# Reordering router, gather and scatter steps around TensorE's work in an attention and mixture-of-experts kernel

## The chip, the cores and the metric

The kernel runs on one core of one Trainium2 chip. The metric is the device time of one execution in microseconds (us). Five engines matter: TensorE (PE, its weight loads shown apart as PEld), VectorE (DVE), ScalarE (ACT), GpSimd (POOL) and SyncE (SP, which here only issues DMAs).

## What is computed

The input is `x` with 8 batches of 1024 tokens of 512 features, in fp32. Two residual steps follow each other:

```
x = x + attention(layernorm(x))      # 16 heads of 32 features; q, k, v are cos/sin of scaled inputs
x = x + moe(layernorm(x))            # 8 experts, 2 per token, at most 160 slots per expert and batch
```

In the attention, q and k are `[cos, sin]` of `x / (1+|w|) + b + t*phi`, v is `cos + sin` of `x / (1+|w|) + b`; the scores are causal and go through a softmax, and the output passes through another `cos + sin`. In the mixture of experts a router (`x @ Wr`, softmax, top 2) gives each token two experts and two gates. Each choice gets a slot, in token order, of its expert and batch; choices past slot 160 are dropped. An expert computes `relu(x @ W1 + b1) @ W2 + b2` (512 to 2048 to 512) on its 8 * 160 = 1280 slots, and each token adds up its two results times their gates.

## The kernel before: how the work is tiled and in which order it runs

**Attention.** The main loop (L1274) runs over n = 0 to 31: batch b = n // 4, and c = n % 4, a chunk of 128 features, which is four heads in two pairs. An iteration prepares q and k for a later chunk, makes the scores of the pairs (`scores`, L658; matmul at L667, exp on ACT at L687), multiplies by v (`attend`, L693; matmul at L701, eviction by DVE at L709) and turns the result back to tokens (`turn`, L725). The order of the instructions on PE, ACT, DVE and SP is written by hand (`manual_schedule`): Python generators are advanced a step at a time, and what is emitted first stands first in the engine's queue. POOL's order is chosen by the framework's own scheduler.

The steps that the change moves:

- `qk_pre(n)` (L492): 16 transposes on PE into a PSUM tile of two banks, and four DVE operations (L508) that scale and add into `qk_f`. The pool of such tiles, `ps_sc`, has three buffers, which scores, router and turns share.
- `v_post(n)` (L622): one DVE product (L436) that writes the v tile; `v_pre` prepares the next one.
- `router(b-1)` (L754) is advanced through batch b's iterations by `route_on`. It makes mean and scale of each token (L765, `inverse_root`), then works on groups g = 0 to 3 of two token tiles: `rows(t)` (L773) normalizes a tile of 128 tokens on DVE (L775) and has SP store it to DRAM (`xn2_d`, L781; its pool `row2` has two buffers); `features(g)` (L786) transposes two rows on PE and copies them out to `xT` (L802 on DVE, L794 on ACT for the last batch) and then calls `rows` for the next group; `sums(g)` multiplies by the router weights (L838), and adds up the parts of the group before (L821). Then come the choice of experts, the counting of places (`mask`, `prior` L903 to L906, matmuls through L821) and `slot` and `token` tiles (L926, L931).
- In the iteration after c == 0, `begin` is true: the router of the batch before starts at the end of iteration c == 0, and `qk_pre` for the next chunk is emitted in the first half of iteration c == 1.

**From router to experts.** `scatter` (L746) writes 16 lists of 128 (token, gate) pairs to `slot_d[b]`, each by an indirect DMA from POOL (L749). `fetch_slots(b)` (L948) reads the slot table back into `slots` (L954). `find_rows(i)` (L1022) turns it into row numbers (`source`), for the first 768 slots of each expert (i = 0, batches 0 to 4) or the other 512 (i = 1). `gather(i)` (L1031) fetches 128 rows at a time by an indirect DMA from POOL (L1037, pool `gp` of two buffers), has PE transpose them (L200 for the first chunk, L1054 later), and forms sums and differences of quarters for Strassen's scheme on DVE.

**Experts.** There are 16 chunks, two per expert (768 and 512 rows). A chunk runs eight `layer1(i, q)` (L1088; seven products each, matmul at L1098) and then two or three `layer2` blocks (L1134; seven products each, matmul at L1143). `mix_w1` (L1074) forms the differences of W1's quarters, on POOL for the first chunk and on DVE later; `mix_w2` (L1001) those of W2 on DVE (L1007 to L1010). `layer2` sends each finished tile of 128 rows to the output by an accumulating indirect DMA from POOL (`send`, L1165). SP loads W1 two steps ahead (`load_ahead`, three buffers) and W2 once per expert.

**The passage between the two.** In the last iteration (n = 31) `experts_begin` (L1199) calls `find_rows(0)`, loads W1 and runs `gather(0)` beside the attention. The last batch's output stage and router (`ending`, L1419) are advanced one step after each layer 1 product of the first chunk, by `next(ending)`. After `layer1(0, 4)` what is left of `ending` is emitted at once, and W2's loads follow on SP. The next chunk's gather is advanced one step after each layer 2 product (`aside`).

Of the kernel before, what the change touches and what calls it, by code (L numbers as in the profile page):

```python
# [21 lines left out]
P = 128  # L22
# [51 lines left out]
def preln_attn_moe_kernel(  # L74
# [667 lines left out]


    scatters = []

    def scatter():  # L746
        while scatters:
            b, idx, src = scatters.pop(0)
            nc.gpsimd.indirect_dma_start(  # L749
                out=slot_d[b], out_offset=bass.IndirectOffsetOnAxis(ap=idx, axis=0),  # L750
                in_=src, in_offset=None,
            )

    def router(b):  # L754

# [7 lines left out]
        mv = small.tile([P, NTT, nc.vector.BN_AGGR_DIM], F32, name="mv")  # L763
        for t in range(NTT):
            nc.vector.bn_aggr(mv[:, t, :], stats[:, t, :, :].rearrange("p c s -> p (c s)"))  # L765
        rstd = inverse_root(mv[:, :, 1], "rstd")

        copy = nc.scalar.copy if b == B - 1 else nc.vector.tensor_copy
        prob = once.tile([P, NTT, E], F32, name="prob")
# [3 lines left out]
        def rows(t):  # L773
# [10 lines left out]
        last = b == B - 1  # L784

        def features(g):  # L786

            xT = row2.tile([P, NCH, 2 * P], F32, name="xT", bufs=1)
            if last:
                for i, xn in enumerate(ahead):  # L790
                    ps = pools["ps_tr"].tile([P, NCH, P], F32, name="ps_t")
                    for c in range(NCH):
                        nc.tensor.transpose(ps[:, c, :], xn[:, c * P : (c + 1) * P], ident)
                    copy(xT[:, :, i * P : (i + 1) * P], ps)  # L794
            else:
                ps = two_banks()
                for i, xn in enumerate(ahead):
                    for c in range(NCH):
                        at = (NCH * i + c) * 64
                        by_halves(ps[:, :, at : at + 64], xn[:, c * P : (c + 1) * P])  # L800
                for a in range(2):
                    copy(  # L802
                        xT.rearrange("p c (i a q) -> p i c a q", a=2, q=64)[:, :, :, a, :],
                        ps[:, a, :].rearrange("p (i c q) -> p i c q", i=2, q=64),
                    )
            if g + 1 < NTT // 2:
                ahead[:] = [rows(2 * g + 2), rows(2 * g + 3)]
                if not last and 2 * g + 4 == NTT:
                    store()
            return xT  # L810

        def one_bank():
            if last:
# [134 lines left out]
    def fetch_slots(b):  # L948

        rows = slot_d[b][: E * CAP, :].rearrange("(e c) k -> c e k", e=E)  # L950
        s0 = b * CAP
        while s0 < (b + 1) * CAP:
            s1 = min((s0 // P + 1) * P, (b + 1) * CAP)
            nc.gpsimd.dma_start(  # L954
                meta[s0 % P : s0 % P + s1 - s0, :, s0 // P, :],
                rows[s0 - b * CAP : s1 - b * CAP],
            )
            s0 = s1


# [70 lines left out]
    def gather(i):  # L1031

        e, j0, nh = chunks[i]
        xe = pools["xep"].tile([P, NCH, 2, HALF], F32, name="xe")
        for j in range(2 * nh):
            xg = pools["gp"].tile([P, D], F32, name="xg")
            nc.gpsimd.indirect_dma_start(  # L1037
                out=xg, out_offset=None, in_=xn2_d[i % 2],
                in_offset=bass.IndirectOffsetOnAxis(ap=source[:, e, j0 + j, None], axis=0),
            )  # L1040
            yield None
            dst = xe[:, :, j // nh, j % nh * P : (j % nh + 1) * P]
            if i == 0:
                ps = two_banks()[:, :, : NCH * 64]
                for c in range(NCH):
                    by_halves(ps[:, :, c * 64 : (c + 1) * 64], xg[:, c * P : (c + 1) * P])
                nc.vector.tensor_copy(
                    dst.rearrange("p c (a q) -> p c a q", a=2),
                    ps.rearrange("p a (c q) -> p c a q", q=64),
                )  # L1050
            else:
                ps = pools["ps_tr"].tile([P, NCH, P], F32, name="ps_t")
                for c in range(NCH):
                    nc.tensor.transpose(ps[:, c, :], xg[:, c * P : (c + 1) * P], ident)  # L1054
# [10 lines left out]
        yield a11, a12, s4, a22, a21, s2, s3  # L1065

    def start(gen, box):
        for box[0] in gen:
            yield
# [4 lines left out]
    def mix_w1(i, q):  # L1074
# [59 lines left out]
    def layer2(i, block, hs, aside):  # L1134
# [27 lines left out]
            )  # L1162

        def send(r):
            nc.gpsimd.indirect_dma_start(  # L1165
                out=out,
                out_offset=bass.IndirectOffsetOnAxis(ap=meta[:, e, jj[r], 0:1], axis=0),
                in_=ys[r], in_offset=None, compute_op=ALU.add,
            )

        p1, u2, u3 = temp("p1"), temp("u2"), temp("u3")
        nc.scalar.copy(p1, product(0, 0))  # L1172
# [26 lines left out]
    def experts_begin():  # L1199

        for name, bufs in (("w1p", 3), ("t1p", 2), ("xep", 1), ("tmp_p", 2), ("gp", 2)):
            pools[name] = to_end.pool(name, bufs, **right)
        find_rows(0)
        for k in range(AHEAD):
            load_ahead(k)
        yield from start(gather(0), first_parts)
        mix_w1(0, 0)

    def experts(ending):
        pools["hp"] = to_end.pool("hp", NHQ, **right)  # L1210
        pools["ps_tr"] = to_end.pool("ps_tr", 2, space=PSUM)
        pools["ps_p"] = to_end.pool("ps_p", 6, space=PSUM)
        box = first_parts
        mixes = loads = iter(())
        for i, (e, j0, nh) in enumerate(chunks):
            parts, box = box[0], [None]
            hs = []
            for q in range(NHQ):
                load_ahead(i * NHQ + q + AHEAD)
                some(3, loads)  # L1220
                if q + 1 < NHQ:
                    mix_w1(i, q + 1)
# [14 lines left out]
            aside = start(gather(i + 1), box) if i + 1 < len(chunks) else iter(())  # L1237
            for block in range(nh):
# [32 lines left out]
    o_st = route = first_rows = None  # L1271
    begin = False
    place, angles, residual = [None], iter(()), iter(())
    for n in range(NCK):  # L1274
# [52 lines left out]
        route_on(1)  # L1327
        route_on(1)
        rest(angles)
        if more:  # L1330
            v_st = v_box[0]
# [9 lines left out]
        if late:  # L1341
            turn(1, halves1, pos)
            o_st = o_pre(n - 1, pos)
        route_on(1)
        if n == 2:
            load_b1()
# [35 lines left out]
        if begin:  # L1382
            rest(residual)
            route = router(b - 1)
            next(route)
        elif n + 2 < NCK:
            qk_st = rest(qk_pre(n + 2))

        if c != 1:
            next(residual, None)  # L1390
        route_on(1)
        if n + 2 < NCK and not begin and c != 1:
            angle(*qk_st)
        if c != 1:
# [24 lines left out]
    def ending():  # L1419
# [4 lines left out]
        square(o_st[0])  # L1424
        for _ in range(3):
            yield
        rest(o_post(NCK - 1, o_st))
        for _ in range(3):
            yield
        for name in router(B - 1):  # L1430
# [39 lines left out]
```

## Time and profile before

| | |
|---|---|
| median of 3 runs | 3331.85 us (3321.11 to 3336.68) |
| the profiled execution: time | 3330.72 us |
| the profiled execution: span | 3329.0 us |
| TensorE busy, share of the span | 3203.4 us, 96% |
| VectorE busy | 2272.0 us, 68% |
| mean granted TensorE clock | 0.990 |
| 0 to 1311 us | attention |
| 1311 to 1412 us | layer 1 of the first chunk, with the last batch's router |
| from 1412 us | layer 2 of the first chunk, then the other 15 chunks |

A line of the timeline gives start, duration, engine, source line, operation, what it writes and reads, its shape and the count of merged instructions; in brackets stands how long the engine was idle before it and what ended that. A line of the waits gives the waiting instruction, what it waited for, the total in us, how often, and the longest. A busy PE may still be slow: its clock can be granted at less than full speed.

### The profile page before, as it was taken

To read this page: it belongs to the slowest core of one execution; us is meant where nothing else is said; L and a number is where in the kernel's file an instruction comes from. 1 tells how busy PE (TensorE), PEld (TensorE's weight loads), DVE (VectorE), ACT (ScalarE), POOL (GpSimd) and SP (SyncE) were. 2 spreads that over 40 slices of the span, in tenths; PEclk is the share of its full clock that TensorE was granted. 3 is DMA by queue.
4 is the path that set the end of the run, shared out by engine and by line. 5 is a ranking of instruction groups with operands and counts; after the bars stand their busy time and mean duration, and the time that the engine had idled before them with its cause. 6 is when DMAs were issued, how large, how long until landed. Compare 5 with 4: busy or idle time off the path is not lost.

```text
span 3329.0 us, 48774 instructions
## 1 busy us (share of the span) xinstructions
PE 3203.4 (96%) x18942; PEld 2172.0 (65%) x18942; DVE 2272.0 (68%) x4975; ACT 1320.9 (40%) x1617; POOL 429.5 (13%) x397
## 2 busy tenths in 40 slices
PE   3999999999999998899999999999999999999998
PEld 1444444444444444588688688688688688688687
DVE  7887878788787675746746846845845845845854
ACT  5788888878787874201101201201201201201201
POOL 2000202020111103321011011011011011011010
PEclk8999999999999999999999999999999999999999
DMA  4445353545535342422322322322322422322321
GB/s 133 117 121 168 106 165 101 167 134 147 174 106 153 87 143 78 126 39 73 111 38 71 114 42 64 117 39 64 117 45 58 121 42 61 119 46 61 114 39 26
DMA packets 234462, 319.74 MB, mean 96 GB/s; under 512 B 21640, under 2 KB 154488, under 8 KB 222200
## 3 DMA queue, kind: packets, MB, share of 16 engines
q1 hardware_dynamic: 211232, 273.37, 27.8%
q0 software_dynamic: 22912, 43.22, 7.4%
q8 instruction: 150, 2.46, 0.3%
q14 instruction: 80, 0.66, 0.1%
q10 hardware_dynamic: 88, 0.02, 0.0%
HBM read 187.62 MB, written 61.82 MB: 75 GB/s over the span
## 4 chain that ended last, share of the span: by engine, by line
PE 59%; DVE 2%; DMA 1%; issue 0%; ACT 0%; POOL 0%; SPq 0%; POOLq 0%; DVEq 0%; ACTq 0%
PE ps_p L1143 28%; PE ps_p L1098 28%; PE av L701 1%; PE ps_t L1054 1%; PE ps_s L667 1%; DMA out_dram<-y,slots 0%; DMA xg<-xn_d,source 0%; DMA xn_d<-xn 0%; DMA w<-in_L_ffn_W_dram 0%; DVE y L1159 0%; PE ps_s L200 0%; DVE w_t L1009 0%; DVE w L1008 0%; DVE t L1083 0%; DVE u L1185 0%
## 5 line engine op out<-in xcount | busy, mean ns | idle before, releaser
L687 ACT ACTIVATE e<-ps_s 128x1024 f32<-128x1024 f32 (+1 forms) x640 | 567.8, 938 | 212.0 <-PE ps_s L667 130.8
L667 PE MATMUL ps_s<-qk 64*128 64x512 f32 (+3 forms) x3072 | 599.4, 508 | 48.5 <-DVE qk_f L508 20.2
L1143 PE MATMUL ps_p<-w,hid 128*128 128x256 f32 x2560 | 569.6, 380 | 0.0
L1143 PEld LDWEIGHTS ps_p<-w,hid 128*128 128x128 f32 x2560 | 484.6, 190 | 66.3
L701 PE MATMUL av<-e,v 128*64 128x512 f32 (+3 forms) x3072 | 526.6, 492 | 0.0
L1143 PE MATMUL ps_p<-w_t,hid 128*128 128x256 f32 x1920 | 430.3, 379 | 0.6 <-DVE w_t L1009 0.6
L667 PEld LDWEIGHTS ps_s<-qk 64*128 64x128 f32 x3072 | 263.3, 189 | 233.3 <-issue 109.4
L1143 PEld LDWEIGHTS ps_p<-w_t,hid 128*128 128x128 f32 x1920 | 361.8, 190 | 48.7 <-DVE w_t L1009 1.0
L701 PEld LDWEIGHTS av<-e,v 128*64 128x64 f32 x3072 | 201.4, 137 | 285.1 <-issue 269.5
L1098 PE MATMUL ps_p<-xe_s,t 128*128 128x256 f32 (+1 forms) x1024 | 299.3, 435 | 4.3 <-DVE t L1083 3.4
L1098 PE MATMUL ps_p<-xe,w 128*128 128x256 f32 (+1 forms) x1024 | 301.8, 438 | 1.1 <-issue 1.1
L1098 PE MATMUL ps_p<-xe,t 128*128 128x256 f32 (+1 forms) x1024 | 296.8, 433 | 0.0
L749 POOL DMA_INDIRECT slot_d<-token,slot x128 | 161.1, 1259 | 1014.1 <-issue 697.3
L1172 ACT COPY p<-ps_p 128x256 f32<-128x256 f32 x40 | 14.8, 369 | 612.9 <-PE ps_p L1143 612.9
L1098 PEld LDWEIGHTS ps_p<-xe_s,t 128*128 128x128 f32 x1024 | 194.4, 191 | 89.4 <-DVE t L1083 7.9
L1098 PEld LDWEIGHTS ps_p<-xe,w 128*128 128x128 f32 x1024 | 194.8, 192 | 83.9 <-issue 4.9
L1098 PEld LDWEIGHTS ps_p<-xe,t 128*128 128x128 f32 x1024 | 194.4, 190 | 80.9 <-issue 0.4
L1037 POOL DMA_INDIRECT xg<-xn_d,source x80 | 78.1, 976 | 1102.8 <-PE ps_t L1054 1020.9
L1165 POOL DMA_INDIRECT out_dram<-y,slots x80 | 126.3, 1579 | 661.8 <-DVE y L1160 522.4
L1113 ACT ACTIVATE p<-ps_p,b_t 128x256 f32<-128x256 f32 (+1 forms) x128 | 65.4, 511 | 330.7 <-DVE y L1159 169.7
L1117 ACT ACTIVATE hid<-hid 128x256 f32<-128x256 f32 (+1 forms) x128 | 60.1, 470 | 321.7 <-DVE hid L1116 321.7
L1130 ACT ACTIVATE hid<-hid,b_more 128x256 f32<-128x256 f32 (+1 forms) x128 | 71.8, 561 | 271.5 <-DVE hid L1129 271.5
(217 smaller groups left out, 3844.8 us busy)
## 6 DMA issues: line engine op xcount, KB each, us to landing
w<-in_L_ffn_W_dram SPq DMA_DIRECT2D x256, 256.0 KB
w<-in_L_ffn_W_dram SPq DMA_DIRECT2D x64, 512.0 KB
qk<-qk_c SPq DMA_DIRECT2D x124, 256.0 KB
qk<-qk_r SPq DMA_DIRECT2D x124, 256.0 KB
qk_base<-base_d SPq DMA_DIRECT2D x28, 1024.0 KB
xn_d<-xn SPq DMA_DIRECT2D x72, 256.0 KB
x_mid<-in_L_attn_x_dram SPq DMA_DIRECT2D x16, 1024.0 KB
out_dram<-x_mid SPq DMA_DIRECT2D x8, 2048.0 KB
```

The lines of the kernel that those rows point to most:

```text
L667: nc.tensor.matmul(ps[:, a, at : at + w], lhsT=pair[r, 1, kb * P : (kb + 1) * P], rhs=pair[r, 0, q0 : q0 + w], start=at == 0, stop=not own ...
L687: nc.scalar.activation(e, ps[:, :, :n], AF.Exp, scale=UNIT * UNIT / math.sqrt(2 * DH))
L701: nc.tensor.matmul(av[a * 64 : (a + 1) * 64, q0 - 512 * h :], lhsT=vt[:, kb, 2 * pr + a, :], rhs=es[i][:, a, at : at + w], start=kb == 0, ...
L749: nc.gpsimd.indirect_dma_start(out=slot_d[b], out_offset=bass.IndirectOffsetOnAxis(ap=idx, axis=0), in_=src, in_offset=None,)
L1037: nc.gpsimd.indirect_dma_start(out=xg, out_offset=None, in_=xn2_d[i % 2], in_offset=bass.IndirectOffsetOnAxis(ap=source[:, e, j0 + j, None ...
L1054: nc.tensor.transpose(ps[:, c, :], xg[:, c * P : (c + 1) * P], ident)
L1098: nc.tensor.matmul(ps, lhsT=weights[:, k, :], rhs=rows[:, k, :], start=k == 0, stop=k == 1)
L1113: nc.scalar.activation(p1, product(b11, a11), AF.Identity, bias=b1_t[:, e * NHC + q : e * NHC + q + 1])
L1117: nc.scalar.activation(h11, h11, AF.Relu)
L1130: nc.scalar.activation(h12, h12, AF.Relu, bias=more)
L1143: nc.tensor.matmul(ps, lhsT=hs[k][:, part, cols], rhs=ws[k][weight], start=k == 0, stop=k == NHQ - 1,)
L1165: nc.gpsimd.indirect_dma_start(out=out, out_offset=bass.IndirectOffsetOnAxis(ap=meta[:, e, jj[r], 0:1], axis=0), in_=ys[r], in_offset=None ...
```

## The change

Seven edits are made together.

1. In the router of batches 0 to 6, the next group's rows leave `features` and become a step of their own, `next_rows`. In the iteration where `begin` is true, the queue order becomes: transposes and copy of group 0, `qk_pre` of q and k, v's product, rows 2 and 3. Later in the same iteration, group 3's features come ahead of the next `qk_pre` and no longer behind it.
2. The last batch's router: statistics, inverse root and first rows become three steps; the output stage is split in two; features start 6 steps after the rows instead of 5, and the place matmuls 5 steps after the counting instead of 1.
3. Scatters of one batch no longer depend on each other; the fetch of the slots depends on all of them.
4. `find_rows(0)` and the first two gathers move to the start of iteration 30, into `row2`'s buffers; the gathers 2 and 3 are requested ahead of the first transpose.
5. The second chunk's `find_rows(1)` moves in front of the W2 mixes, and its gather starts in block 0 (after two products), with POOL's order fixed.
6. W1's eighth tile is loaded before b2 and W2; POOL mixes W1 only for q < 6 in the first chunk, DVE the last two; the PSUM pools of the experts wait by tile.
7. In `layer2` product (4, 3) comes ahead of (6, 5), so that `send(0)` stands after five products instead of six.

```diff
 def scatter():
     while scatters:
         b, idx, src = scatters.pop(0)
+        ins = nc.gpsimd.indirect_dma_start(
...
+        for other in scattered[b]:
+            tc.declare_no_dep(ins, other, reason="rows of their own")
+        scattered[b].append(ins)
...
-            if g + 1 < NTT // 2:
-                ahead[:] = [rows(2 * g + 2), rows(2 * g + 3)]
-                if not last and 2 * g + 4 == NTT:
-                    store()
             return xT
+        def next_rows(g):
+            ahead[:] = [rows(2 * g + 2), rows(2 * g + 3)]
+            if not last and 2 * g + 4 == NTT:
+                store()
...
             xT = features(g)
+            if g + 1 < NTT // 2:
+                if not last:
+                    yield
+                next_rows(g)
             yield
...
+            for other in scattered[b]:
+                tc.add_manual_dep(
...
 def gather(i):
+        there = []
+        if i == 0:
+            there = [fetch(row2.tile([P, D], F32, name="xn2"), j) for j in range(2)]
             yield None
+            there += [fetch_next(j) for j in (2, 3)]
+        xe = pools["xep"].tile([P, NCH, 2, HALF], F32, name="xe")
+        for j in range(2 * nh):
+            if len(there) == j:
+                there.append(fetch_next(j))
+            if j or i:
+                yield None
+            xg = there[j]
...
+                if 1 < j and j + 2 < 2 * nh:
+                    there.append(fetch_next(j + 2))
...
-        mix = nc.gpsimd.tensor_tensor if i == 0 else TT
+        mix = nc.gpsimd.tensor_tensor if i == 0 and q < 6 else TT
...
         TT(u2, p1, product(5, 4), ALU.add)
+        p5 = product(4, 3)
+        TT(p1, u2, p5, ALU.add)
+        TT(p1, p1, p3, ALU.add)
+        gated(0, 1, p1)
+        send(0)
         TT(u3, u2, product(6, 5), ALU.add)
-        p5 = product(4, 3)
-        TT(u2, u2, p5, ALU.add)
-        TT(u2, u2, p3, ALU.add)
-        gated(0, 1, u2)
-        send(0)
...
-        pools["ps_p"] = to_end.pool("ps_p", 6, space=PSUM)
+        pools["ps_p"] = to_end.pool("ps_p", 6, space=PSUM, reuse_waits="tile")
...
-                load_ahead(i * NHQ + q + AHEAD)
+                if i or q != NHQ - AHEAD - 1:
+                    load_ahead(i * NHQ + q + AHEAD)
...
+                    load_ahead(NHQ - 1)
                     load_b2(0)
                     rest(load_w2(0))
...
+            if i == 0:
+                find_rows(1)
             rest(mixes)
             aside = start(gather(i + 1), box) if i + 1 < len(chunks) else iter(())
+            if i == 0:
+                aside = behind(2, aside)
             for block in range(nh):
-                if i == 0 and block == 1:
-                    find_rows(1)
-                layer2(i, block, hs, aside if i or block else iter(()))
+                layer2(i, block, hs, aside)
...
+        if n == NCK - 2:
+            find_rows(0)
+            next(first_gather)
...
             qk_st = rest(qk_pre(n + 1))
+            if begin:
+                v_post(n, v_st)
+                next(route)
             angle(*qk_st)
...
         elif n + 2 < NCK:
+            route_on(1)
             qk_st = rest(qk_pre(n + 2))
...
-        if more:
+        if more and not begin:
             v_post(n + 1, v_st)
...
-        rest(o_post(NCK - 1, o_st))
-        for _ in range(3):
-            yield
+        for _ in o_post(NCK - 1, o_st):
+            yield
+        yield
         for name in router(B - 1):
-            for _ in range(5 if name == "tiles" else 1):
+            for _ in range({"tiles": 6, "places": 5}.get(name, 1)):
                 yield
```

More of the change, by code (lines that the diff above doesn't have):

```diff
@@ L744, in preln_attn_moe_kernel @@
     scatters = []
+    scattered = {b: [] for b in range(B)}
     def scatter():
@@ L748, in scatter @@
             b, idx, src = scatters.pop(0)
-            nc.gpsimd.indirect_dma_start(
+            ins = nc.gpsimd.indirect_dma_start(
                 out=slot_d[b], out_offset=bass.IndirectOffsetOnAxis(ap=idx, axis=0),
                 in_=src, in_offset=None,
-            )
+            ).ins
+            for other in scattered[b]:
+                tc.declare_no_dep(ins, other, reason="rows of their own")
+            scattered[b].append(ins)
     def router(b):
@@ L765, in router @@
             nc.vector.bn_aggr(mv[:, t, :], stats[:, t, :, :].rearrange("p c s -> p (c s)"))
+        last = b == B - 1
+        if last:
+            yield
         rstd = inverse_root(mv[:, :, 1], "rstd")
+        if last:
+            yield
         copy = nc.scalar.copy if b == B - 1 else nc.vector.tensor_copy
@@ L782, in rows @@
             return xn
-        last = b == B - 1
         def features(g):
@@ L953, in fetch_slots @@
             s1 = min((s0 // P + 1) * P, (b + 1) * CAP)
-            nc.gpsimd.dma_start(
+            ins = nc.gpsimd.dma_start(
                 meta[s0 % P : s0 % P + s1 - s0, :, s0 // P, :],
                 rows[s0 - b * CAP : s1 - b * CAP],
-            )
+            ).ins
+            for other in scattered[b]:
+                tc.add_manual_dep(
+                    ins, other.name,
+                    mybir.DependencyInfo(
+                        mybir.DependencyClass.Sync, mybir.DependencyReason.DATA
+                    ),
+                    reason="rows of all scatters",
+                )
             s0 = s1
@@ L1033, in gather, with fetch @@
         e, j0, nh = chunks[i]
[L1034 to L1037, printed above, removed]
+        def fetch(xg, j):
+            ins = nc.gpsimd.indirect_dma_start(
                 out=xg, out_offset=None, in_=xn2_d[i % 2],
@@ L1040, in gather, with fetch_next @@
             )
-            yield None
+            if i in (1, 2):
+                tc.keep_in_program_order(ins)
+            return xg
+        def fetch_next(j):
+            return fetch(pools["gp"].tile([P, D], F32, name="xg"), j)
+        there = []
+        if i == 0:
+            there = [fetch(row2.tile([P, D], F32, name="xn2"), j) for j in range(2)]
+            yield None
+            there += [fetch_next(j) for j in (2, 3)]
[6 more added lines that the diff above has]
+            xg = there[j]
             dst = xe[:, :, j // nh, j % nh * P : (j % nh + 1) * P]
@@ L1065, in gather, with behind @@
         yield a11, a12, s4, a22, a21, s2, s3
+    def behind(count, gen):
+        for _ in range(count):
+            yield
+        yield from gen
     def start(gen, box):
@@ L1164, in send @@
         def send(r):
-            nc.gpsimd.indirect_dma_start(
+            ins = nc.gpsimd.indirect_dma_start(
                 out=out,
@@ L1169, in send @@
             )
+            if i == 0:
+                tc.keep_in_program_order(ins)
         p1, u2, u3 = temp("p1"), temp("u2"), temp("u3")
@@ L1202, in experts_begin @@
             pools[name] = to_end.pool(name, bufs, **right)
-        find_rows(0)
         for k in range(AHEAD):
             load_ahead(k)
-        yield from start(gather(0), first_parts)
+        yield from start(first_gather, first_parts)
         mix_w1(0, 0)
@@ L1210, in experts @@
         pools["hp"] = to_end.pool("hp", NHQ, **right)
-        pools["ps_tr"] = to_end.pool("ps_tr", 2, space=PSUM)
-        pools["ps_p"] = to_end.pool("ps_p", 6, space=PSUM)
+        pools["ps_tr"] = to_end.pool("ps_tr", 2, space=PSUM, reuse_waits="tile")
+        pools["ps_p"] = to_end.pool("ps_p", 6, space=PSUM, reuse_waits="tile")
         box = first_parts
@@ L1235, in experts @@
                     next(mixes)
+            if i == 0:
+                find_rows(1)
             rest(mixes)
             aside = start(gather(i + 1), box) if i + 1 < len(chunks) else iter(())
+            if i == 0:
+                aside = behind(2, aside)
             for block in range(nh):
-                if i == 0 and block == 1:
-                    find_rows(1)
-                layer2(i, block, hs, aside if i or block else iter(()))
+                layer2(i, block, hs, aside)
             rest(aside)
@@ L1273, in preln_attn_moe_kernel @@
     place, angles, residual = [None], iter(()), iter(())
+    first_gather = gather(0)
     for n in range(NCK):
@@ L1326, in preln_attn_moe_kernel @@
         rest(residual)
-        route_on(1)
-        route_on(1)
+        for _ in range(3):
+            route_on(1)
         rest(angles)
@@ L1343, in preln_attn_moe_kernel @@
             o_st = o_pre(n - 1, pos)
+        route_on(1)
         route_on(1)
@@ L1386, in preln_attn_moe_kernel @@
         elif n + 2 < NCK:
+            route_on(1)
             qk_st = rest(qk_pre(n + 2))
@@ L1390, in preln_attn_moe_kernel @@
             next(residual, None)
-        route_on(1)
         if n + 2 < NCK and not begin and c != 1:
@@ L1426, in ending @@
             yield
-        rest(o_post(NCK - 1, o_st))
-        for _ in range(3):
+        for _ in o_post(NCK - 1, o_st):
             yield
+        yield
         for name in router(B - 1):
-            for _ in range(5 if name == "tiles" else 1):
+            for _ in range({"tiles": 6, "places": 5}.get(name, 1)):
                 yield
```

## The prediction

> **What bounds the kernel now.** I read the page's busy shares and its chain first, then what TensorE waited for, then the timelines of TensorE, VectorE and POOL around the longest of these waits.
>
> ```profile
> PE 3203.4 (96%) x18942; PEld 2172.0 (65%) x18942; DVE 2272.0 (68%) x4975; ACT 1320.9 (40%) x1617; POOL 429.5 (13%) x397
> ```
>
> TensorE is busy 96% of the span, so a faster other engine is worth nothing by itself. What can be won is the rest, 126 us, of which 47 lie in the first 60 us, untouched here, plus the time in which a busy TensorE runs slowly. In 1500 to 3200 us it idles 2.6 us in all. So the change can act in two places only: the attention's router iterations, and 1258 to 1450 us.
>
> ```profile
> PE ps_s L667 <- DVE qk_f L508: 20.2, 7, 7.7
> PE ps_s L838 <- DVE xT L802: 6.6, 8, 0.8
> PE ps_t L1054 <- DMA xg<-xn_d,source: 4.2, 1, 4.2
> PE ps_t L821 <- DVE prior L904: 3.5, 1, 3.5
> ```
>
> The first row is seven waits, 7.7 us of it at 61 us in iteration 0 and six in the router iterations; the second has the waits of the groups' features. TensorE in the first router iteration:
>
> ```profile
> 254.35 1.99 PE L667 MATMUL ps_s<-qk 64*128 64x512 f32 x8 [1.63 <-DVE qk_f L508]
> ...
> 260.79 0.62 PE L838 MATMUL ps_s<-xT,wr_sb 128*32 128x256 f32 x8
> ...
> 285.85 0.64 PE L838 MATMUL ps_s<-xT,wr_sb 128*32 128x256 f32 x8 [0.82 <-DVE xT L802]
> ```
>
> VectorE in the same stretch, without a pause from 246.8 to 262.1:
>
> ```profile
> 247.68 1.22 DVE L436 SCALAR_TENSOR_TENSOR v<-v_p,t_r 128x1024 f32<-128x1024 f32 x1
> 248.81 0.74 DVE L709 TENSOR_SCALAR av_sb<-av,inv_o 128x512 f32<-128x512 f32 x1
> 249.48 1.28 DVE L802 COPY xT<-ps_s 128x512 f32<-128x512 f32 x2
> 250.67 0.99 DVE L775 TENSOR_SCALAR xn<-x_mid,mv,rstd 128x512 f32<-128x512 f32 x2
> 251.58 2.71 DVE L508 SCALAR_TENSOR_TENSOR qk_f<-ps_s,inv_qk,qk_base 128x512 int32<-128x512 f32 x4
> ...
> 259.00 1.28 DVE L802 COPY xT<-ps_s 128x512 f32<-128x512 f32 x2
> ```
>
> The scores at 254.35 need the buffer that L508 frees at 254.3. But the second xT copy ends at 260.2, and TensorE asks for it at 260.79: a slack of 0.6 us only. TensorE in the passage:
>
> ```profile
> 1270.66 0.69 PE L200 MATMUL ps_s<-ident,xg 64*128 64x64 f32 x8 [1.79 <-DMA xg<-xn_d,source]
> ...
> 1342.39 1.02 PE L821 MATMUL ps_t<-gather_e,lg 128*128 128x8 f32 x4 [2.35 <-ACT xT L794]
> ...
> 1370.41 0.66 PE L821 MATMUL ps_t<-mask,before 128*128 128x64 f32 x2 [3.51 <-DVE prior L904]
> ...
> 1372.22 4.93 PE L1098 MATMUL ps_p<-xe,w 128*128 128x384 f32 x8
> ...
> 1447.99 0.92 PE L1054 MATMUL ps_t<-ident,xg 128*128 128x128 f32 x4 [4.20 <-DMA xg<-xn_d,source]
> ```
>
> The eight matmuls at 1372.22 take 4.93 us where the same eight take 2.74 later: a wait is followed by slow matmuls. POOL:
>
> ```profile
> 1426.79 1.07 POOL L749 DMA_INDIRECT slot_d<-token,slot  x1 [1.44 <-DMA slot_d<-token,slot]
> 1429.27 0.96 POOL L749 DMA_INDIRECT slot_d<-token,slot  x1 [1.42 <-DMA slot_d<-token,slot]
> 1431.66 1.58 POOL L954 DMA_DIRECT2D slots<-slot_d  x2 [1.42 <-DMA slot_d<-token,slot]
> ```
>
> Each scatter waits for the landing of the one before.
>
> [...] x2 in duration after 1370, and none after the 1.63 us wait at 254. [...] the scatters land 2.1 us after issue at best, 3.0 in the median. [...] L1131 takes 1.76 us at 1403.7, beside POOL's W1 mix, against 0.56.
>
> **The sum, part by part** (against the profiled execution, 3330.72 us with its 3329.0 of span, 1.1 below the median of the runs; the load of 1.7 us around the span stays).
>
> *Attention, edit 1.* v's product (1.13 from start to start) and rows 2 and 3 (0.91) go behind L508. VectorE then waits for `av`, which TensorE ends at 248.24, and so idles 0.56; L508 ends at 248.24 + 0.67 + 1.19 + 2.72 = 252.8 instead of 254.3, and TensorE gains 0.53 (a wait at 250.9 on xT) + 1.5 = 2.0 there. What is late next: the copy of group 1's xT. VectorE has the same work ahead of it as before, plus the 0.56, so it ends at 260.75, and TensorE starts group 1's sums at about 260.8 as before. The stall moves; nothing is gained. This holds in four batches. In the three where rows 2 and 3 also waited for the store of rows 0 and 1 in front of L508 (VectorE idle 1.03, 1.33 and 0.54 + 0.94 for "DMA xn_d<-xn"), that wait falls away, since the store gets L508's and v's 4 us more, and the slow matmuls with it. Group 1's copy then comes 0.65, 0.77 and 0.92 us sooner (those pauses less the 0.56) and ends at 414.4, 1032.8 and 878.0, where TensorE asked for it only at 417.1, 1035.5 and 879.0: 2.7 + 2.7 + 1.0 = 6.4. Group 3's features in front of `qk_pre` end the wait of 0.82 in all seven: 5.7; L508 comes 1.3 later there, and VectorE has pauses of 0.9 and 3.9 us to take it. SP's row stores are issued 4 us later, with nothing behind them but a load a microsecond long. Sum: -12.
>
> *Gather 0, edit 4.* Waits of 2.54 + 0.51 + 1.79 = 4.8 and about 3 us of slow matmuls after them. The first two rows are now there before. Gathers 2 and 3 still need `gp`'s memory, which q's and k's last transfers free at 1256.5, and landed 5.2 to 5.6 us after issue beside W1's loads; the fourth lands 3.3 after TensorE's third transpose. I leave 3 us of waits: -4.5. POOL's order here is the scheduler's; one mix of 0.72 in front costs that much.
>
> *Start of layer 1, edit 6.* The first product waits 1.13 for the turn's PSUM banks and runs slowly for 1.8 more; by tile: -2.
>
> *Last router, edit 2.* Waits of 1.69 + 1.90 + 2.35 = 5.9, slow time after them 3.4. Rows 2 and 3 waited for stores (VectorE idle 1.45), VectorE's lateness held ACT's copies. With six products (7.7 us) between, the store of 4.6 us is over. Rows 4 to 7 still come two products after the last: I leave 2 us: -7.
>
> *Place matmuls, edit 2.* 3.51 + 0.67 + 2.6 slow; five products are 6.5 us, VectorE needs 1.6 for the counting: -6.5. The tokens come six products later in the queue, as one program step in layer1(0, 4)'s last product.
>
> *W1 mixes and W1 before W2, edit 6.* The wait of 0.85 at 1405 for POOL's mix goes: -0.85. VectorE takes on 8 x 0.43 = 3.4 us; a layer of 9.03 us has eleven operations of 0.47 and 0.7 us of ACT's, so 3.1 to spare. W2's eight loads wait for layer1(0, 4) (9 us later than now) and take 13 us at a full DMA; they are first needed 18 us after. No cost; uncovered, at most the excess over 5 us.
>
> *Scatters, gather 1, edits 3 and 5.* Two indirect DMAs without a wait follow in 1.35 us: 16 make 21.6, instead of 51.2 (1378.0 to 1429.3). With the last landing (3.0) and the slots' (3.4) they are there 28 us after the first. VectorE comes to `find_rows(1)` 27.1 (three layers) + 4.2 (its lag at 1411.6) - 2 (token's lag) = 29.3 after. So the new wait, with all W2 mixes and layer 2's evictions behind it, costs nothing, with 1 us to spare. The mixes still end 10 us later, so the 0.64 at 1425.8 stays. The gather then is requested 10 us before its transpose: 4.20 and 1.8 slow fall: -6.
>
> *send(0) one product sooner, edit 7.* TensorE's end is not moved. At the end, send(1) waits from 3318.5 to 3321.4 for send(0)'s landing, which comes 3.45 us sooner: -2.8.
>
> Sum: -12 - 4.5 - 2 - 7 - 6.5 - 0.85 - 6 - 2.8 = -41.7: 3289.0, and 3290 for a median.
>
> **The rivals.** *VectorE has the slack after all* in the router iterations, say because group 1's copy overtakes: then all of 24.8 us of waits and 3 of slow time go, 16 more: 3274. Against it: VectorE's unbroken line. *VectorE bounds the first chunk*: it has 8 x 5.9 us of layers, 5.8 of output stage, 16 of router and 6.8 of mixes, 76 in all, for TensorE's 82 (56 products of 1.29, the router's 8.5, a slow start), and starts 4 late; the 13.5 of the last router and places come back as waits for rows or evictions: 3303. *The scatters stay one after the other* (the queue's own semaphores, say): the slots land 57 us after the first scatter, `find_rows(1)` holds VectorE for 28: 3317. *Slower*: the same wait with scatters as slow as batch 4's (67 us, and 4 for the slots) beside W2's loads (13): 84 - 29 = 55 us before the W2 mixes: 3344. It decides from slots later than 71 us after the first scatter.
>
> **How the numbers follow.** Forecast 0.55, its own range 3280 to 3299; VectorE's slack 0.14; VectorE as the bound 0.17; serial scatters 0.09; slower 0.05. A measurement can tell about 0.5% (16.7 us) from no change: the first three are faster, 0.86; serial scatters are the same, 0.09. The range reaches from the first rival to past the second, with 6 us for what stays open in gathers and slots: 3272 to 3310.
>
> **What would show it.** Right: no wait for L508 in the router iterations, but one of about 2 us for xT L802 or lg L843 at group 1's sums; no 0.82 at group 3; scatters 1.3 us apart; no wait for prior L904 and none at the first L1054; the last send right behind its data. Wrong: VectorE idle ahead of L1026 behind the slots, or TensorE waits of over 5 us in the first chunk.

## The result, and the profile after

The changed kernel took 3371.07 us (median of four runs, 3361.70 to 3379.14), the kernel before 3331.39 us beside it (3321.11 to 3336.68): a ratio of 1.0132, 95% interval 1.0109 to 1.0155. It is slower by 40 us where 42 us less were forecast. The profiled execution took 3361.70 us, with a span of 3359.9 us.

The result hangs on more than the kernel: the same program took 3307.93 us in a later group of runs, 0.9947 of the kernel before (0.9928 to 0.9966). The experiments show what differs.

The page's line of busy time, of the changed kernel:

```profile
PE 3216.5 (96%) x18942; PEld 2172.4 (65%) x18942; DVE 2258.3 (67%) x4983; ACT 1322.3 (39%) x1617; POOL 423.8 (13%) x389
```

TensorE has the same 18942 matmuls and is busy 13 us longer: part of the loss hides in its busy time, as matmuls at a lower clock (granted 0.94 from 1145.3 to 1351.7 us, beside 0.98 in the same part of the kernel before, 1123.0 to 1311 us). Its waits (total, times, longest):

```profile
PE ps_s L667 <- ACT e L687: 18.6, 11, 5.1
...
PE ps_s L667 <- DVE qk_f L508: 11.9, 9, 7.9
PE ps_s L667 <- issue: 10.3, 9, 2.1
PE ps_s L667 <- DVE rec L736: 9.3, 3, 6.4
...
PE ps_s L847 <- DVE xT L810: 5.5, 7, 0.8
PE ps_s L667 <- DVE prob L854: 4.0, 7, 0.6
```

The wait for L508 has shrunk from 20.2 to 11.9. The one in iteration 0 makes 7.9 of it, and 0.55 is left in each of the seven router iterations, where the forecast had none. The "issue" and L736 rows are new, and that for L687 has grown from 10.3 to 18.6; the forecast had none of these. TensorE in the first router iteration, in its timeline:

```profile
249.35 1.99 PE L667 MATMUL ps_s<-qk 64*128 64x512 f32 x8 [0.55 <-DVE qk_f L508]
...
256.14 0.31 PE L830 MATMUL ps_s<-gather_e,lg 128*32 128x8 f32 x16 [0.43 <-DVE lg L852]
257.24 0.64 PE L847 MATMUL ps_s<-xT,wr_sb 128*32 128x256 f32 x8 [0.79 <-DVE xT L810]
```

The stall moved for the most part from L508 to group 1's sums, as forecast: 0.43 + 0.79, where "about 2 us" was written down. The passage, in the same view:

```profile
1351.71 2.82 PE L1144 MATMUL ps_p<-xe,w 128*128 128x384 f32 x8 [1.12 <-issue]
...
1377.85 1.08 PE L847 MATMUL ps_t<-xT,wr_sb 128*32 128x256 f32 x8 [2.65 <-ACT xT L802]
...
1412.16 0.43 PE L830 MATMUL ps_t<-prior,ones 128*128 128x64 f32 x2 [0.67 <-DVE prior L919]
...
1475.20 0.63 PE L1094 MATMUL ps_t<-ident,xg 128*128 128x128 f32 x4 [1.89 <-DMA xg<-xn_d,source]
```

The 3.51 for the places is gone. So is the 4.20 at gather 1's first transpose, but its fourth now waits 1.89. From layer 1's first product to layer 2's the first chunk takes 91.0 us (1351.7 to 1442.7) instead of 100.6. And yet layer 1 begins 40.7 us later than before, at 1351.7 instead of 1311.05. The loss lies in the attention: from the first scatter of batch 0 to that of batch 5 the kernel before needs 774.8 us (348.2 to 1123.0), the changed one 800.9 (344.5 to 1145.3). Each of the five batches in between holds one run of 16 scatters. From batch 6's first scatter to layer 1 another 14.0 us are lost (37.2 instead of 23.2). POOL's timeline there:

```profile
1314.53 0.99 POOL L751 DMA_INDIRECT slot_d<-token,slot  x1 [17.11 <-DVE token L944]
1315.82 0.97 POOL L751 DMA_INDIRECT slot_d<-token,slot  x1 [0.30 <-issue]
1317.10 0.96 POOL L751 DMA_INDIRECT slot_d<-token,slot  x1 [0.30 <-issue]
```

They come every 1.26 us, to 1334.5. VectorE, ScalarE and TensorE meanwhile, each in its timeline:

```profile
1317.50 0.75 DVE L709 TENSOR_SCALAR av_sb<-av,inv_o 128x512 f32<-128x512 f32 x1 [2.60 <-PE av L701]
1330.10 0.26 DVE L736 RECIPROCAL rec<-ps_s 128x16 f32<-128x16 f32 x1 [11.85 <-remote]
```

```profile
1321.65 1.02 ACT L687 ACTIVATE e<-ps_s 128x1024 f32<-128x1024 f32 x1 [0.65 <-PE ps_s L200]
1337.19 0.60 ACT L687 ACTIVATE e<-ps_s 128x512 f32<-128x512 f32 x1 [14.52 <-remote]
```

```profile
1319.51 0.66 PE L200 MATMUL ps_s<-ident,av_sb 64*128 64x64 f32 x16
...
1322.72 2.08 PE L667 MATMUL ps_s<-qk 64*128 64x512 f32 x4 [0.89 <-ACT e L687]
1331.23 2.08 PE L667 MATMUL ps_s<-qk 64*128 64x512 f32 x4 [6.42 <-DVE rec L736]
```

The reciprocal L736 needs only the 16 transposes L200, and in the program it waits on TensorE's semaphore alone. TensorE ends them at 1320.2; VectorE, with nothing else to do, begins at 1330.1. "Remote" says that no instruction ended near the raise of the semaphore that released it. The raise itself is in the trace, which keeps the time at which each semaphore rose: TensorE's rose at 1330.07, 9.9 us after the transposes ended, and next at 1337.11 to 1337.23, when ScalarE goes on with scores whose last matmul had ended at 1321.8. ScalarE's own semaphore rose within 0.02 us of the end of each exp here, and TensorE starts 0.05 us after the exp that ends at 1322.67. So what is late is the signal that TensorE has finished, and not the two engines or every signal. The profile models the ends of matmuls, so a late end and a late signal of it can't be told apart; TensorE had begun later matmuls meanwhile, at 1321.05 and 1322.72.

ScalarE stands for 14.5 us, and TensorE, which needs both, idles 6.42 and then runs at half clock (2.08 for four matmuls that took 1.13 at 1317.38; the granted clock was 0.50 from 1331.0 to 1333.4). In the kernel before no such wait for "remote" appears.

### The profile page after: what moved, and what is told of

The parts are those of the page before. It is cut to its first block, busy times and chain, and to the rows that moved or that the text cites. A ratio compares the mean times of both kernels' runs of the same rounds, so it can differ in the third digit from the quotient of the medians.

```text
span 3359.9 us, 48793 instructions
## 1 busy us (share of the span) xinstructions
PE 3216.5 (96%) x18942; PEld 2172.4 (65%) x18942; DVE 2258.3 (67%) x4983; ACT 1322.3 (39%) x1617; POOL 423.8 (13%) x389
## 4 chain that ended last, share of the span: by engine, by line
PE 82%; DVE 9%; ACT 3%; issue 2%; DMA 2%; another core or an unknown queue 1%; SPq 0%; POOL 0%; POOLq 0%; DVEq 0%; ACTq 0%
PE ps_p L1189 27%; PE ps_p L1144 26%; PE av L701 14%; PE ps_s L667 12%; ACT e L687 2%; PE ps_s L200 1%; PE ps_s L681 1%; DVE qk_f L508 1%; PE ps_t L1094 1%; DVE qk_r L436 1%; DVE v L436 0%; DMA xn<-in_L_attn_x_dram 0%; DVE xT L810 0%; DMA xg<-xn_d,source 0%
## 5 line engine op out<-in xcount | busy, mean ns | idle before, releaser
L667 PE MATMUL ps_s<-qk 64*128 64x512 f32 (+3 forms) x3072 | 607.5, 511 | 69.7 <-ACT e L687 18.6
L687 ACT ACTIVATE e<-ps_s 128x1024 f32<-128x1024 f32 (+1 forms) x640 | 569.0, 938 | 261.3 <-PE ps_s L667 126.8
L1189 PEld LDWEIGHTS ps_p<-w_t,hid 128*128 128x128 f32 x1920 | 361.9, 190 | 51.2 <-DVE w_t L1030 3.6
L1159 ACT ACTIVATE p<-ps_p,b_t 128x256 f32<-128x256 f32 (+1 forms) x128 | 65.5, 512 | 332.4 <-PE ps_p L1144 172.8
```

The lines of the kernel that those rows point to most:

```text
L667: nc.tensor.matmul(ps[:, a, at : at + w], lhsT=pair[r, 1, kb * P : (kb + 1) * P], rhs=pair[r, 0, q0 : q0 + w], start=at == 0, stop=not own ...
L687: nc.scalar.activation(e, ps[:, :, :n], AF.Exp, scale=UNIT * UNIT / math.sqrt(2 * DH))
L1159: nc.scalar.activation(p1, product(b11, a11), AF.Identity, bias=b1_t[:, e * NHC + q : e * NHC + q + 1])
L1189: nc.tensor.matmul(ps, lhsT=hs[k][:, part, cols], rhs=ws[k][weight], start=k == 0, stop=k == NHQ - 1,)
```

## The experiments

Theory H1: the dense runs of scatters (edit 3) hold TensorE's completion signals back from VectorE and ScalarE; without them the change gains. H2: the new order of edit 1 makes the batches slower. H3: `find_rows(1)` and the pinned order of edit 5 cost it in the passage. The runs came in five groups, each on one chip and with the kernel before beside it.

### First group: which edit (kernel before 3331.68)

**e1**, scatters one behind another again:

```diff
-            for other in scattered[b]:
-                tc.declare_no_dep(ins, other, reason="rows of their own")
```

> The changed kernel with its scatters one behind another again, the slots' fetch and every other edit as changed. H1 (the dense burst of scatters keeps TensorE's completion signals from VectorE and ScalarE, six batches cost 5.5 us each and the passage to layer 1 another 13): the bursts' cost of 45 to 55 us goes, 3371 less about 50, so 3320, down to 3300 if the passage doesn't lose what edit 3 gave it, up to 3340 if find_rows(1) now waits for the last scatter with the W2 mixes behind it. In the trace the batches take 155 us again and no remote wait over 2 us stands at a rec or an exp. H2 (the new order of edit 1 makes the batches slower): 3362 to 3385, batches still 160 us. H3 (find_rows(1) and the pinned order in the passage cost it): 3371 or more, up to 3400.

**e2**, side by side in the last batch alone:

```diff
-            for other in scattered[b]:
+            for other in (scattered[b] if b == B - 1 else []):
                 tc.declare_no_dep(ins, other, reason="rows of their own")
```

> The changed kernel with side by side scatters for the last batch alone, one behind another for the other seven. H1: the batches' loss of 33 us goes and the passage keeps its short scatters, 3371 less 33 to 45, so 3330 with 3315 to 3338; below the kernel before or level with it. Under H1 the difference to the serial run says what the last burst costs (TensorE idle only 1.3 us in it) against what find_rows(1) would wait. H2: 3362 to 3375. H3: 3362 to 3375.

**e3**, meant to keep two under way:

```diff
-            for other in scattered[b]:
+            for other in scattered[b][-1:]:
```

> The changed kernel with each scatter free of the one just before it only, so that two are under way at a time. H1 with the number under way or the issue rate deciding: between the serial run and the changed kernel, 3330 to 3355, the bursts some 30 us long. If only a queue that never empties does the harm, near 3371; if only many at once do, near the serial run. H2 and H3: 3362 to 3375, as all the others.

**e4**, the kernel before with edit 3 alone:

```diff
-            nc.gpsimd.indirect_dma_start(
+            ins = nc.gpsimd.indirect_dma_start(
...
+            for other in scattered[b]:
+                tc.declare_no_dep(ins, other, reason="rows of their own")
...
+                tc.add_manual_dep(
```

> The kernel before with edit 3 alone (scatters free of each other, the slots' fetch behind all of them). H1: each of seven bursts adds 5 to 7 us, 3331 plus 35 to 50, so 3373 with 3360 to 3390. H2 and H3: 3326 to 3333, since no path of the kernel before waits long for a scatter.

Measured: e1 3338.27 us (ratio 1.0019, 1.0007 to 1.0031), e2 3311.77 (0.9949, 0.9933 to 0.9964), e3 3370.20 (1.0121, 1.0099 to 1.0144), e4 3394.05 (1.0185, 1.0161 to 1.0208). e3 told nothing new on the number under way: its program is, instruction for instruction, the changed kernel, and so it serves as that kernel in this group. H2 and H3 fall: edit 3 alone makes the kernel before 62 us slower, which is more than the range expected of e4, and the changed kernel without it in seven batches is faster than the kernel before, and under the range expected of it. The first seven batches' edit 3 costs 3370.2 - 3311.8 = 58.4 us, 8.3 a batch. In e4 some of the loss has another cause. From the last batch's first scatter to the end it takes 1958.0 us, the kernel before 1951.0: the last 16 scatters stand on POOL in front of its W1 mixes, and TensorE waits 4.48 us for one (6.36 in e15, below). In the changed kernel, whose last two mixes are VectorE's, no such wait appears.

The last batch's is worth e1 less e2, 26.5 us. VectorE and TensorE of e1:

```profile
1423.61 0.18 DVE L1045 TENSOR_SCALAR source<-slots 128x32 int32<-128x32 int32 x1 [28.70 <-DMA slots<-slot_d]
```

```profile
1425.11 1.22 PE L1187 MATMUL ps_p<-w_t,hid 128*128 128x256 f32 x2 [24.45 <-DVE w_t L1028]
```

With serial scatters `find_rows(1)` holds VectorE 28.70 us and the W2 mixes behind it, for which the prediction's rival with serial scatters had 28, and TensorE waits 24.45.

### Second group: what in a dense run does it (kernel before 3327.08)

**e5**, two POOL additions behind each scatter of the first seven batches:

```diff
             scattered[b].append(ins)
+            for _ in range(2 if b < B - 1 else 0):
+                    nc.gpsimd.tensor_tensor(fill, fill, fill, ALU.add)
```

> The changed kernel, scatters free of each other in all batches, but in the first seven two POOL additions of 128x256 stand behind each scatter (0.72 us each beside the mixes), so that one is issued every 2.7 us as in the serial order, with none waiting for another. H1 with the density of issue as the cause: the bursts are 43 us long and cost nothing, so the time of the run with side by side scatters in the last batch alone, 3312, with 3305 to 3320. If it is not the density but that no scatter waits for the one before: 3360 to 3375. If POOL's work between them does harm of its own: above 3325.

**e6**, e2 with extra gathers ahead of the serial scatters; **e7** and **e8** with direct DMAs there, of POOL and of SP:

```diff
+        for b, idx, src in scatters:
+            if b < B - 1:
+                    nc.gpsimd.indirect_dma_start(
+                        out=dumt[:, len(dumn) % 16, :], out_offset=None, in_=scr_d,
...
+                    nc.gpsimd.dma_start(scr_d[n_ * P : (n_ + 1) * P, :], src)
...
+                    nc.sync.dma_start(scr_d[n_ * P : (n_ + 1) * P, :], src)
```

> The kernel with side by side scatters in the last batch alone, and in each of the first seven batches 16 extra indirect gathers of 128 rows of 8 bytes from a DRAM buffer into SBUF, nothing waiting for them, right ahead of its serial scatters. If any dense run of POOL's indirect DMAs keeps TensorE's signals back: 3312 plus 45 to 65, so 3357 to 3377. If it takes writes to DRAM: 3310 to 3318.

> As the gather run, but with 16 extra direct DMAs of POOL in each of the first seven batches, each writing 128 rows of 8 bytes to a DRAM buffer that nothing reads. If the harm comes from POOL's way of issuing DMAs in general, or from many small writes to DRAM: 3350 to 3377. If it takes the indirect form: 3310 to 3320.

> As the run with POOL's direct DMAs, but SP issues them: the same 16 times 128 rows of 8 bytes to DRAM, without POOL. If small writes to DRAM do the harm: 3350 to 3377. If POOL's issuing does it: 3310 to 3322, the upper end since loads of the next batch stand behind them on SP's queue.

Measured: e5 3328.62 (1.0003, 0.9992 to 1.0013), e6 3327.63 (1.0002, 0.9992 to 1.0012), e7 3325.03 (0.9997, 0.9988 to 1.0006), e8 3364.37 (1.0120, 1.0101 to 1.0139). None shows a "remote" wait. e6 and e7 fell between the two ranges expected of each. e6's batches 0 to 5 take 153 to 154 us as in e2; its loss is one wait of 13.3 us for POOL's W1 mix, which stood behind batch 6's later scatters. In e5 a batch takes 156 to 157 us, 3 more than in e2; that this is the additions is likely, but not tested apart. e8 is slow for another reason, seen in its VectorE:

```profile
524.06 1.23 DVE L427 TENSOR_SCALAR qk_r<-qk_f 128x2048 int32<-128x2048 int32 x1 [5.86 <-DMA qk<-qk_r]
```

SP took 8.18 us to issue the 16 transfers, and q's and k's moves stood behind them. These runs seemed to show that pacing is enough, and to clear reads and direct DMAs. The later groups showed that they can't tell.

### Third and fourth group: the same programs, two answers (kernel before 3327.36 and 3332.68)

**e9** and **e10**, e2 with 16 extra scatters in the first six batches, of rows of 8 and 512 bytes; **e11**, meant as groups of four:

```diff
+            if b < B - 2:
+                ins = nc.gpsimd.indirect_dma_start(
+                    out=scr_d, out_offset=bass.IndirectOffsetOnAxis(ap=idx, axis=0),
+                    in_=src, in_offset=None,
...
+                    in_=ident, in_offset=None,
```

```diff
-            for other in scattered[b]:
+            k = len(scattered[b])
+            for other in scattered[b] if b == B - 1 else scattered[b][k - k % 4 :]:
```

> The kernel with side by side scatters in the last batch alone, and in each of the first six batches 16 extra indirect scatters of 128 rows of 8 bytes, free of each other, into a DRAM buffer that nothing reads, right ahead of its serial scatters: the twin of the gather run, with writes for reads. H1 (a dense run of scatters keeps TensorE's signals back, nothing else of the changed kernel is needed): batches of 158 to 163 us instead of 153.5 and remote waits at e L687 or rec L736, so 3312 plus 30 to 50, 3342 to 3362. If the harm needs the removed dependences or the data's later use: 3310 to 3318.

> As the twin, but each of the 128 rows is 512 bytes long (from the identity matrix). If it is small writes to DRAM that do the harm: batches near 153.5 to 155, 3310 to 3322. If it is the indirect scatter as such: as the twin with 8 bytes, 3342 to 3362 or more.

> The changed kernel, but in the first seven batches the scatters are free of each other in groups of four, and each group's first waits for all before it. If the harm grows with the length of the dense run, so that a pause of 1.4 us every fifth microsecond clears it: near 3312, up to 3325. If each scatter without a wait costs the same: three quarters of 59 us, so 3350 to 3360.

Measured: e9 3312.66 (0.9950, 0.9932 to 0.9968), e10 3312.67 (0.9954, 0.9939 to 0.9968), e11 3307.61 (0.9936, 0.9917 to 0.9956). That contradicted H1. The extra runs of e9 are as dense as the changed kernel's, 1.26 us apart. So are e11's: the program put the scatters in an order in which the waits between fours were already met. Either order and waits decided, or where the runs were made. So the changed kernel (e12), e11 (e13), e9 (e14) and e4 (e15) ran together, unaltered:

> The changed kernel once more, beside the groups of four and the twin burst on one chip. If order and waits of the scatters decide: 3371 as before, 3362 to 3379, with remote waits from 7.5 us after a burst's start. If the chip decides: it may be near 3310 here, and then the groups of four and the twin are too.

> The groups of four once more. If order and waits decide: 3308, 3304 to 3312. If the chip decides and this one is of the kind on which dense bursts do harm: 3350 to 3375.

> The twin burst of 8 byte rows into an unread buffer once more. If it matters that the scatters write the buffer of the slots: 3313. If the chip decides: with the changed kernel, both slow (3342 to 3362 here) or both fast.

> The kernel before with edit 3 alone once more. If order and waits decide: 3394, 3385 to 3405. If the chip decides and this one does no harm: 3325 to 3332, level with the kernel before.

Measured: e12 3375.95 (1.0137, 1.0120 to 1.0154), e13 3368.93 (1.0118, 1.0098 to 1.0138), e14 3366.18 (1.0099, 1.0082 to 1.0116), e15 3395.19 (1.0194, 1.0176 to 1.0211). The fours went from 3307.61 to 3368.93, the twin from 3312.66 to 3366.18, with nothing edited. And e14 shows that a dense run of scatters into a buffer that nobody reads does the harm by itself: 54.4 us over e2 of the first group for six runs, with waits for "remote" at L688 of 30.9 us in total. One of them, in e14's ScalarE:

```profile
526.85 1.94 ACT L688 ACTIVATE e<-ps_s 128x1024 f32<-128x1024 f32 x2 [7.06 <-remote]
```

### Fifth group: the changed kernel once more (kernel before 3326.32)

**e16** is the changed kernel; **e17** and **e18** are e6 and e7 with `b < B - 2` for `b < B - 1`.

> The changed kernel a third time, as the control of its chip. Harmful kind: 3362 to 3380. Harmless kind: level with the groups of four there, 3304 to 3314, some 0.6% below the kernel before.

> The gather burst in the first six batches alone (the sixth and last but one left out, where the serial scatters behind it held POOL's mixes). On a harmful chip, if any dense run of POOL's indirect DMAs does harm: 3355 to 3370, as the twin with scatters. If only writes do: 3310 to 3316. On a harmless chip: 3310 to 3316, which tells nothing new.

> POOL's 16 direct DMAs of 128 rows of 8 bytes in the first six batches alone. On a harmful chip, if POOL's DMAs in general or small writes do harm: 3345 to 3370. If it takes the indirect form: 3312 to 3322 (the later loads of q's and k's rows cost the rest). On a harmless chip: 3312 to 3322.

Measured: e16 3307.93 (0.9947, 0.9928 to 0.9966), e17 3314.57 (0.9966, 0.9954 to 0.9977), e18 3319.33 (0.9973, 0.9964 to 0.9982). The place of batch 6's scatters in e16, VectorE, ScalarE and TensorE:

```profile
1280.52 0.26 DVE L736 RECIPROCAL rec<-ps_s 128x16 f32<-128x16 f32 x1 [1.96 <-PE ps_s L200]
```

```profile
1280.28 2.56 ACT L687 ACTIVATE e<-ps_s 128x1024 f32<-128x1024 f32 x3
```

```profile
1282.27 1.99 PE L667 MATMUL ps_s<-qk 64*128 64x512 f32 x8
```

The same instructions that stood 11.85, 14.52 and 6.42 us at the first measurement waited 1.96, 0 and 0 us, beside scatters that are as dense.

What tells the two kinds of places apart:

| | kernel before | changed kernel | batch 0 to 1, changed | TensorE idle + lost to the clock in it |
|---|---|---|---|---|
| result; groups 1, 4 | 3331.4; 3331.7, 3332.7 | 3371.1; 3370.2 (e3), 3376.0 | 162.9 (result) | 9.50 + 3.41 |
| groups 3, 5 | 3327.4, 3326.3 | 3307.9 (group 5) | 153.3 (e16) | 2.86 + 0 |

"Batch 0 to 1" runs from first scatter to first scatter; the clock's loss is the time under half clock, halved (the granted clock was 0.98 over it in the result's profile). The 9.6 us between the rows are 6.6 of waits and 3.4 of clock, less 0.4. There is a second sign. I counted, in each trace, the instructions of TensorE, VectorE and ScalarE that raise their engine's semaphore, some 8080, and the raises on record. In the changed kernel of the result and in all eight runs of groups 1 and 4, 56 to 147 fewer raises than instructions are on record, even in e1 (56), whose serial scatters lose no time; in all ten runs of groups 2, 3 and 5 it is at most one fewer, and in the profile of the kernel before none. Those that are missing lie in or just behind the runs of scatters: in e12, 707 of 803 are on record there, and outside none is missing.

A third sign is how late TensorE's raises are. In the result and in the six runs of groups 1 and 4 with dense runs in the first batches, 48 to 60 of them are on record over 0.3 us after the last end of an instruction that makes them; in e1 and e2 13 and 18, none over 1.3 us; in the kernel before and in groups 2, 3 and 5 none. VectorE's and ScalarE's raises are that late nowhere (the last two of each engine at the end of every span are left out). So H1 holds at the harmful places: the signals that come late are TensorE's. The second group was of the harmless kind. So e5 doesn't tell whether the density of the scatters matters or that none waits for the one before, and e6, e7, e17 and e18 don't tell whether gathers or direct DMAs do harm on the other.

What makes a place harmful stays open. Groups 4 and 5 have the same chip number, so the number does not tell it, and what is called a place here may as well be the time of the runs. Raises are missing on record in just these stretches. Whether the recording itself has a part in TensorE's lateness was not shown: no run tests it, and whether an execution without any record loses the time isn't known. Missing raises alone are no measure of lost time: in e12 more than a third of them lie at the last batch's run, which costs TensorE little (in the changed kernel at the first measurement 1.25 us of waits, below).

## Why the prediction was wrong

**The step that failed** is "Scatters, gather 1, edits 3 and 5". It says "16 make 21.6, instead of 51.2", and that came true: 20.8 us at the last batch (1419.35 to 1440.15). But it priced this for the last batch alone. The other seven runs got no term, and no reason was given for that. They are the whole loss at a harmful place: 58.4 us (e3 less e2). The rival that was to end slower took the same edit and had the wrong mechanism: `find_rows(1)` waited 0.58 us in the changed kernel at the first measurement, not 28 or 55. No row of before shows a scatter without a wait, so this was an operation that the trace doesn't show, and its cost had to be bounded from above too.

**The sum was more than twice too large as well.** At a harmless place the change gives 3307.93 - 3326.32 = -18.4 instead of -41.7; e2 gives -19.9 at a harmful one. e16 and the profile of before (spans 3307.3 and 3329.0) share it out. Where the profile of before was taken isn't on record, so the two may differ in kind of place too. The first 4.2 us, up to the first scatter, are mostly chance: with edit 3 alone, which alters nothing there, that point comes at 345.0 and 344.5 (e4, e15), beside 348.2 and e16's 343.9. For the rest:

| term | forecast | measured, e16 |
|---|---|---|
| attention, first scatter of batch 0 to batch 5 | -10.5 of the -12 | -5.3 |
| to batch 6, with gather 0 | -4.5 - 0.8 | -3.5 |
| from batch 6 to the end | -25.2 | -8.7 |

- *Attention.* In the three batches with a wait for the row stores the intervals fell by 2.8, 0.6 and 3.0: 6.4, for 6.4 of that cause; the other two changed by +1.6 and -0.5. The -5.7 for group 3's features failed: the 0.82 goes, but the scores then wait 0.57 for prob L854 in each of seven batches, a step that I didn't ask "what is late next" of.
- *Gather 0.* Waits of 4.84 became 1.33 + 3.19. The cover of the early requests was right for two rows and wrong for the others, as the "3 us of waits" allowed. The view puts the 1.33 down to POOL's mix, but TensorE's queue stood until 1253.1 for gather 2, which was issued at 1247.36 and landed at 1253.06.
- *Start of layer 1.* The wait of 1.13 stayed at 1.13; only the slow matmuls behind it went (4.51 to 2.82), and not by this edit: without it e4 and e15 have 2.82 too, and with it e6 has 4.51.
- *Last router and places.* 5.94 became 4.10: 1.44 for layer 1's own hid L1162, which stands on VectorE behind the router's statistics and first rows, and 2.66 for ScalarE's copy of these two rows, held by VectorE's lateness. The later rows, for which 2 us were left, cost no wait. The places' 4.18 became 0.67.
- *W2 mixes.* This "costs nothing, with 1 us to spare" missed by 2.8 us:

```profile
1394.98 0.18 DVE L1047 TENSOR_SCALAR source<-slots 128x32 int32<-128x32 int32 x1 [2.41 <-DMA slots<-slot_d]
```

```profile
1401.62 0.70 PE L1189 MATMUL ps_p<-w_t,hid 128*128 128x256 f32 x2 [1.01 <-DVE w_t L1030]
```

  In e16 the slots' fetch starts 5.8 us after the last scatter and not 3.0, VectorE waits 2.41 and TensorE 0.74 + 1.01 + 1.01 + 0.65 = 3.41 for the mixes, where it had waited 0.64.
- *Gather 1.* The 4.20 at its first transpose went, but its fourth waits 1.67 instead of nothing; and the gather behind it, which cost nothing before, waits 1.91 (at 1548.1).
- *Tail.* From TensorE's end to the span's end 11.78 became 9.12: -2.7, for -2.8.

The waits from layer 1's start to gather 1 fell from 16.9 to 11.0 us, where the forecast left 2.6 (2 for the last router, 0.64 for the mixes). Most waits that were named shrank or went. The first product's stayed, and that for the W2 mixes grew; what was left out is for the most part what came late next.

**The better version** is e2: 20 us less than the kernel before at a harmful place. It was not run at a harmless one by itself; with an unread run of scatters added (e9) it took 3312.66 there, 0.9950. It keeps the last batch's dense run, which costs this kernel little even at a harmful place: from its first scatter to the end the changed kernel took 1940.6 us at the first measurement and 1942.0 in e16. TensorE's signals are late there too, as its VectorE shows at the first measurement:

```profile
1442.13 0.56 DVE L1162 TENSOR_TENSOR hid<-p,ps_p 128x384 f32<-128x384 f32 x1 [1.92 <-PE ps_p L1144]
```

ScalarE's L1159 waits 3.09 us just before it, and neither waits in e16. But TensorE has other products to run meanwhile and waits only 1.25 us for L1162.

## What to carry to other kernels

Taking a wait away where nobody waits for the result was not free here: it made a trickle of DMAs (2.36 us apart or more) a burst (1.26 us apart), and in the first group the bursts of seven batches cost 58.4 us (e3 less e2). Let only those transfers go side by side whose end someone waits for, as e2 does (0.9949). When the same program gives two times, run it again beside its control before explaining it by an edit: here two groups of experiments would have told a false story.

## What the runs showed of the hardware

- Beside sixteen indirect DMAs of 128 rows each, 1.26 us apart, a raise of TensorE's semaphore came 9.9 us (VectorE idle 11.85) and another some 15 us (ScalarE idle 14.52) after the end of the work that it tells of (changed kernel, first measurement, from 1314.53); ScalarE's own raises came within 0.02 us in the same stretch. With DMAs 2.36 us apart or more, each behind the landing of the one before, no raise of TensorE's stood more than 1.0 us behind the last end of an instruction that makes one at the same place (e1; up to 5.3 by this measure in the changed kernel), and the batches took 153 to 154 us.
- Whether the time is lost differs between groups of runs: 3370 to 3376 us (result, e3, e12) or 3308 (e16) for one program, while the kernel before differs by some 5 us (3331 to 3333, 3326 to 3327).
- SP took 8.18 us to issue 16 transfers of 128 rows of 8 bytes (e8, at 503.44), 0.51 each; the moves of q and k behind them on its queue were issued from 511.73 on.
